# Set 1 of the first mixture as rows by expert, group choice by rank, and a new order of stages

## The chip, the cores and the metric

The kernel runs on one core of a Trainium2 chip. Its time is the device time of one launch in microseconds (us), and the figure compared is the median over several launches. TensorE is called PE here, VectorE DVE, ScalarE ACT, GpSimd POOL, and SyncE SP. SP only issues transfers; ACT and POOL issue some as well.

## The reference

`x` is 32 sequences of 128 positions with 128 features, in f32: 4096 tokens. Six layers are added to it one after the other, each on a layer norm of `x`. The first and the second are an attention and a cross-attention to `ctx`, the fourth and the fifth another attention (with random features) and another cross-attention. The third and the sixth are mixtures of 16 experts:

```python
# third layer: experts of width 64, four groups of four experts
scores = sigmoid(x2d @ router_weight.T)
sc = scores + e_bias
group_scores = sum of the two greatest sc of each group
# only the two best groups count; of them the 4 greatest sc are chosen
tw = 2.5 * scores[chosen] / (sum(scores[chosen]) + 1e-20)
routed = sum over the 4 chosen e of tw_e * (silu(x @ gate_e.T) * (x @ up_e.T)) @ down_e.T
out = routed + shared          # shared: one MLP of width 128 for all tokens

# sixth layer: experts of width 128, the 4 greatest logits, softmax over them, plus a shared MLP
```

## The kernel before

The tokens are eight groups of four sequences (512 tokens). Two groups make a set: set 0 is groups 0 and 1, set 3 is groups 6 and 7. `x` stays on the chip, as [128 positions, 4, 128 features] per group. `fast_decoder` (L960) has four stages: `first_layers` (L1667) with both first attentions of all groups and the experts of group 0 of the first mixture; `mixture_layer` (L2031) with the first mixture of groups 1 to 7; `second_layers` (L2664) with both later attentions; and `last_layer` (L2239) with the second mixture.

**An order written by hand.** `steps` (L1219) takes a list of small pieces of work (a stage, its first step, every how many steps, and how often). Step by step it takes one instruction group from each stage in the order of the list, and between them one from the `between` list. The result is the order of each engine's own queue, and an engine works through it in that order: an instruction that waits holds all behind it on its engine. The order of a list thus decides which queue holds what ahead of what.

**The first mixture, dense.** For each group, `norm`, `scaled` and `turn` make the normalized tokens, once by rows and once turned with the features on partitions (`hx`). `routing` (L1904) computes the router's logits of a set, and `route_groups` (L1797) turns them into weights: sigmoid, the sums of all pairs in each expert group, then `pick` (L1757) for the two best groups and again for the four best experts. `pick` takes the greatest element out k times, six DVE operations each time, breaking ties by a table. The weights go through `send` (L1919) to memory and `fetch` (L1933) brings them back spread over all partitions, four transfers of 512 KB a group. `experts` (L1947) then takes nine chunks per group: eight of two experts (2 x 64 = 128 wide) and the shared MLP. A chunk is three matmuls (`pg`, `pu`, `y`) of 128x512, a Silu on ACT (L1960), and two products on DVE: with `pu` (L1961) and with the spread weights, the share (L1963). The dense chunks compute all 16 experts for all tokens. At most two chunks are in flight, since `pg` and `pu` have four PSUM banks. The sum `y` is copied, turned back (`pyt`) and added to `x`.

**The second mixture.** Its sets 0, 2 and 3 go as rows by expert, through `Tables` (L2089): `route` (L2123) finds the four experts of each token; `placed` (L2160) computes for each token and choice a row in a table in memory, so that the rows of one expert stand together, padded to tiles of 128 rows; `owned` (L2218) finds each tile's expert. `way_out` (L2224) writes the normalized rows to their places: 32 indirect transfers of 128 rows for a set, issued by POOL. Then come 11 quads of four tiles. `rows_of` (L2288) reads a quad's rows and its experts' weights on SP's queue, `rows_turned` (L2304), `rows_up` (L2317) and `rows_down` (L2328) compute them and write the results to a second table. `way_back` (L2337) gathers each token's four results, 32 indirect transfers for a set on POOL, and `added` (L2347) adds them to `x` with their weights on DVE. Set 1 is dense there. Both tables are filled beforehand (`filled`, L2084). At the end `chunk_down` (L2367) computes the last group's shared MLP, adds `x` in the same PSUM sum, copies the 128x512 result (L2378) and sends it out.

**Names in the middle.** While the first mixture ends, pieces of the next attention start: the list `also` (L2031 on). One of them computes on POOL the squares `y2` (L2548), on which the first features of that attention (PE) wait. SP has one queue for all its loads, here: the later weights (L997), `share` (L1943), the weights sent to memory (L1931), and the second mixture's weights (L1026).

Of the kernel before, what the change touches and what calls it, by code (L numbers as in the profile page):

```python
# [9 lines left out]
F32 = mybir.dt.float32  # L10
# [7 lines left out]
GB = 4  # L18
# [57 lines left out]
def _layout(i):  # L76
# [9 lines left out]
    signs, scales = i["L1_attn_sorf_signs"], i["L1_attn_sorf_scales"]  # L86
    pad = lambda a: np.concatenate([a, np.zeros((128 - len(a), a.shape[1]), a.dtype)], 0)
# [68 lines left out]
            "sd": i["L0_ffn_sh_down_w"].T,  # L156
        },
# [802 lines left out]
def fast_decoder(ctx: ExitStack, tc: tile.TileContext, ins, spans, out: bass.AP):  # L960
# [322 lines left out]
    NU = NG * GB  # L1283

# [382 lines left out]
    def first_layers(after):  # L1667
# [15 lines left out]
        rscaled_, rnorm_ = first(rscaled), first(rnorm)  # L1683
        of_four = lambda stage, b, at: (lambda g: stage(g * GB + b), at, 4, NG)
# [3 lines left out]
        def early_keys(s):  # L1688
            for _ in range(early_at[s]):
# [4 lines left out]
        steps(  # L1694
            (lambda k: xvalues(2 * k + 1), 11, 2, NW),
            (weights, 4, 1, NU),
            (lambda k: xvalues(2 * k), (5, 12), 2, EARLY - 1),
            (lambda w: xproject("k", w + EARLY), 8 + 2 * EARLY, 2, NW - EARLY),
# [3 lines left out]
            (lambda g: average(g * GB + GB + 3), 12, 4, NG - 1),  # L1702
            (xweights, (9, 11), 1, NU),
            (finish_, 12, 4, NG - 1),
            of_four(average, 2, 7),
            of_four(average, 0, 5),
            (lambda _: fetch_inside(wk), 41, 1, 1),
            (lambda k: xvalues(2 * (k + EARLY - 1)), 8 + 2 * EARLY, 2, NW - EARLY + 1),
            (first(rturn), 24, 4, NBR // GB),
# [5 lines left out]
            (next_two(rturn), 39, 1, NBR // GB, rscaled_later),  # L1715
            (inside, 42, 1, 2),
            (lambda _: average(3), 7, 1, 1),
            (turn, (3, 7, 11), 4, NG, head_norms),
            (first(send), 39, 1, 1, choose),
            (first(routing), 29, 1, 1),  # L1720
            (finish_first, 7, 1, 1),
            (head_squares, (2, 5, 10), 4, NG, head_means),
            of_four(average, 1, 6),
            (xfinish_b, 13, 2, NW),
            (lambda _: routing(wk, 1), 40, 1, 1),
            (inside, 42, 1, 3),
            (inside, 42, 1, 3),
            (inside, 42, 1, 3),
            (xaverage, (9, 11), 1, NU),
            (xshare, 11, 2, NW),  # L1730
            between=[
                (rnorm_later, 37, 1, NBR // GB),
                (rscaled_later, 38, 1, NBR // GB),
                (xfinish_c, 14, 2, NW),
                (norms, (0, 1, 8, 12), 4, NG),
                (lambda _: choose(1, 12), 41, 1, 3),
                (head_norms, (3, 6, 11), 4, NG),
                (head_means, (2, 5, 10), 4, NG),
                (xnorm, (7, 12), 4, NG, finish_first, finish_),
                (rscaled_, 23, 4, NBR // GB),  # L1740
                (scaled, (1, 2, 9), 4, NG),
                (lambda _: load_w0f(), 21, 1, 1),
                (xscaled, (8, 13), 4, NG),
                (biased, 1, 4, NG),
                (rnorm_, 22, 4, NBR // GB),
                (xnormalize, 12, 2, NW, xweights),
                (lambda k: load_late(LATE[k]), (17, 18), 1, len(LATE)),
                (lambda _: choose(0, 5), 30, 1, 11),
                (filled, 16, 1, NT // 4),
# [6 lines left out]

    def pick(v, n, k, desc):  # L1757

        m = v.shape[1]
        eq = st.tile([128, m, n], F32, name=f"eq{n}", bufs=2)  # L1760
        top = st.tile([128, m], F32, name=f"top{n}", bufs=2)
        for _ in range(k):
            nc.vector.tensor_reduce(top, v, AX.X, ALU.max)
            yield
            nc.vector.tensor_tensor(eq, v, rep(top, n, 2), ALU.is_equal)
            yield
            nc.vector.tensor_tensor(eq, eq, rep(desc, m, 1), ALU.mult)
            yield
            nc.vector.tensor_reduce(top, eq, AX.X, ALU.max)
            yield  # L1770
            nc.vector.tensor_tensor(eq, eq, rep(top, n, 2), ALU.is_equal)
            yield
            nc.vector.scalar_tensor_tensor(v, eq, -BIG, v, ALU.mult, ALU.add)
            yield

    def picked(v):

        nc.vector.tensor_scalar(v, v, -0.1 * BIG, None, ALU.is_lt)
# [18 lines left out]
    def route_groups(lg, wk):  # L1797

        s = wk.tile([128, NBR, E], F32, name="s", bufs=1)
# [14 lines left out]
        yield from pick(gs, 4, 2, K["desc4"])  # L1814
        picked(gs)
# [3 lines left out]
        yield from pick(v, E, 4, K["desc16"])  # L1819
        picked(v)  # L1820
# [10 lines left out]
        comb = wk.tile([128, NBR, E], F32, name="comb", bufs=1)  # L1831
# [19 lines left out]
    def route_softmax(lg, wk):  # L1851

        s = wk.tile([128, NBR, E], F32, name="s", bufs=1)
# [25 lines left out]
        comb = wk.tile([128, NBR, E], F32, name="comb", bufs=1)  # L1879
        nc.vector.tensor_tensor(comb, v, rep(den, E, 2), ALU.mult)  # L1880
        yield
        return comb

    def mixture(tag, W, route, per, last, weights_of, more={}, kept=lambda g: None):
# [14 lines left out]
        def turn(wk, g):  # L1899
            pool, bufs = (edge, 2) if g in groups(0) else (wk, 5)  # L1900
            hs[g] = more[g] if g in more else pool.tile([128, GT], F32, name="hx", bufs=bufs)
            by_feature(xn.pop(g), hs[g])
# [6 lines left out]
        def choose(n, some=-1):  # L1909

            try:
                while some:
                    next(choices[n])
                    some -= 1
            except StopIteration as end:
                if end.value is not None:
                    combs[n] = end.value
# [907 lines left out]
```

## Time and profile before

| what | us |
|---|---|
| median of 11 runs | 1313.91 |
| lowest and highest of them | 1310.22, 1323.21 |
| the profiled execution | 1306.24 |
| its span | 1304.5 |

The stretches of that execution, with the busy time of the engines in each:

| stage | stretch, us | PE | DVE | ACT | POOL | DMA share |
|---|---|---|---|---|---|---|
| first layers | 0 to 597 | 554.7 | 409.6 | 275.5 | 211.8 | 0.24 |
| first mixture, groups 1 to 7 | 597 to 780 | 180.4 | 116.2 | 52.7 | 23.6 | 0.38 |
| second layers | 780 to 1048 | 241.4 | 196.7 | 155.0 | 134.0 | 0.06 |
| second mixture | 1048 to 1304.5 | 229.4 | 132.3 | 106.0 | 165.1 | 0.69 |

Busy time is the time in which an engine executes; a stage lasts as long as its longest chain of waits. The DMA share is the mean busy share of the core's 16 DMA engines. A releaser (`<-`) is the instruction whose end let a waiting one start.

### The profile page before, as it was taken

The numbers are of one execution on the slowest core, as the hardware profiler recorded it, in microseconds if no ns is written. First come the engines' busy times: TensorE is split into PE (matmuls) and PEld (weight loads), VectorE is DVE, ScalarE is ACT, GpSimd is POOL, SyncE is SP. The second block draws the span as 40 slices with busy tenths as digits, with TensorE's granted clock in tenths as the row PEclk, the third lists the DMA queues.
The fourth block names the chain that finished last, engine by engine and source line by source line (L and its number), as shares of the span: only waits on it lengthen the run. The fifth ranks groups of instructions, "written<-read, shape, count | busy, mean of one in ns | idle before, by whom it ended". The sixth has DMA issues, their size and how long they took to land. (4 is left out here: it accounts for less than half of the span.)

```text
span 1304.5 us, 27090 instructions
## 1 busy us (share of the span) xinstructions
PE 1205.8 (92%) x10586; PEld 802.2 (61%) x10586; DVE 854.8 (66%) x2298; ACT 589.2 (45%) x883; POOL 534.5 (41%) x715
## 2 busy tenths in 40 slices
PE   7679999999999999988999998999997788999996
PEld 5357667777777777643443445667665446787753
DVE  5756767686868667576775555688888565524662
ACT  4545454554545443333232224667664433554431
POOL 6244252435352213214000013555543747477774
PEclk9889999999999999999999999999999889999998
DMA  9401221111111112417362301000000157898823
GB/s 327 140 2 34 86 86 34 34 34 34 34 34 34 35 44 57 99 35 163 62 131 57 75 25 80 2 2 2 2 2 8 35 200 263 291 327 282 278 72 94
DMA packets 82751, 118.62 MB, mean 91 GB/s; under 512 B 9016, under 2 KB 57784, under 8 KB 81208
## 3 DMA queue, kind: packets, MB, share of 16 engines
q1 hardware_dynamic: 70280, 92.95, 25.4%
q0 software_dynamic: 6144, 12.60, 3.1%
q10 hardware_dynamic: 6192, 11.26, 2.3%
q8 instruction: 86, 1.41, 0.5%
q14 instruction: 49, 0.40, 0.1%
HBM read 89.71 MB, written 27.07 MB: 90 GB/s over the span
## 5 line engine op out<-in xcount | busy, mean ns | idle before, releaser
L1311 ACT ACTIVATE e<-scores 128x1024 f32<-128x1024 f32 x128 | 124.0, 1021 | 85.4 <-PE scores L981 85.4
L981 PE MATMUL y<-sg,wide 128*128 128x512 f32 x206 | 109.6, 623 | 14.4 <-DVE sg L2365 7.4
L2340 POOL DMA_INDIRECT back<-rows_out,place x96 | 93.4, 973 | 31.1 <-issue 23.5
L1149 POOL TENSOR_SCALAR xn<-x,mv,r 128x128 f32<-128x128 f32 x78 | 69.3, 894 | 84.9 <-PE pxn L1158 79.9
L1565 ACT ACTIVATE e<-xscores 128x1024 f32<-128x1024 f32 x64 | 62.0, 1021 | 65.2 <-PE xscores L981 65.2
L1120 POOL TENSOR_SCALAR r<-mv 128x4 f32<-128x4 f32 x46 | 14.4, 315 | 184.7 <-DVE mv L1139 184.6
L1326 DVE STREAM_TRANSPOSE by_token<-sums 128x512 f32<-128x512 f32 x64 | 45.5, 711 | 66.4 <-PE sums L981 66.1
L1120 POOL TENSOR_SCALAR r2x<-mv 128x2 f32<-128x2 f32 x16 | 3.7, 234 | 203.4 <-DVE mv L1139 203.4
L1960 ACT ACTIVATE sg<-pg 128x512 f32<-128x512 f32 x63 | 37.6, 597 | 107.0 <-PE pg L981 99.1
L981 PE MATMUL scores<-qb,k 32*128 32x512 f32 x512 | 74.7, 654 | 11.2 <-ACT e L1311 7.1
L1961 DVE TENSOR_TENSOR sg<-sg,pu 128x512 f32<-128x512 f32 x63 | 43.2, 686 | 53.3 <-PE pu L981 53.1
L981 PE MATMUL sums<-e,v 128*32 128x128 f32 x2048 | 74.4, 288 | 0.5 <-ACT e L1311 0.5
L981 PEld LDWEIGHTS y<-sg,wide 128*128 128x128 f32 x206 | 34.1, 193 | 63.5 <-DVE sg L1963 29.3
L981 PEld LDWEIGHTS sums<-e,v 128*32 128x32 f32 x2048 | 56.4, 115 | 24.9 <-issue 10.6
L981 PE MATMUL po<-e,v 128*64 128x128 f32 x1024 | 64.9, 277 | 3.8 <-DVE v L1579 3.8
L1613 ACT COPY av<-po 128x512 f32<-128x512 f32 x64 | 37.6, 587 | 64.3 <-PE po L981 63.3
L981 PE MATMUL pqk<-h,wide 128*128 128x256 f32 x256 | 64.5, 397 | 0.7 <-ACT h L1161 0.7
L981 PE MATMUL pval<-wide,ctx 128*128 128x512 f32 x128 | 63.1, 615 | 1.8 <-DVE by_token L1326 1.8
L981 PEld LDWEIGHTS po<-e,v 128*64 128x64 f32 x1024 | 55.1, 137 | 12.3 <-issue 4.2
L1544 DVE COPY qk<-pqk 128x512 f32<-128x512 f32 x54 | 36.8, 685 | 35.6 <-PE pqk L981 35.4
L981 PE MATMUL pu<-hx,wide 128*128 128x512 f32 x116 | 59.3, 593 | 0.0
L981 PE MATMUL pqk<-ctx,wide 128*128 128x256 f32 x256 | 59.3, 384 | 0.0
(355 smaller groups left out, 2955.3 us busy)
## 6 DMA issues: line engine op xcount, KB each, us to landing
row_weights<-in_w1f_dram SPq DMA_DIRECT2D x99, 192.0 KB
factor<-factors SPq DMA_DIRECT2D x64, 256.0 KB
share<-combined SPq DMA_DIRECT2D x28, 512.0 KB
rows_in<-in_few SPq DMA_DIRECT2D x33, 256.0 KB
rows<-rows_in SPq DMA_DIRECT2D x33, 256.0 KB
rows_out<-yrows ACTq DMA_DIRECT2D x33, 256.0 KB
share<-combined SPq DMA_DIRECT2D x8, 1024.0 KB
wide<-in_w1f_dram SPq DMA_DIRECT2D x1, 3272.0 KB
```

What stands on the lines that cost most here:

```text
L981: last[0] = nc.tensor.matmul(*args, **kw)
L1120: nc.gpsimd.tensor_scalar(t, src, add, None, ALU.add)
L1149: eng.tensor_scalar(n[:, b, :], x[g][:, b, :], mv[:, b, 0:1], r[:, b : b + 1], ALU.subtract, ALU.mult)
L1311: nc.scalar.activation(e[-1], ps[:, bass.ts(n, 2)].rearrange("p c i s -> p (c i) s"), AF.Exp, scale=scale)
L1326: nc.vector.transpose(tt.rearrange("p i t r -> p (i t r)"), po.rearrange("p i s -> p (i s)"))
L1544: nc.vector.tensor_copy(t, ps)
L1565: nc.scalar.activation(e[-1], ps[:, n].rearrange("p r c s -> p (r c) s"), AF.Exp, scale=scale)
L1613: nc.scalar.copy(avs[w][n][:, :, bass.ts(b, S)], po)
L1960: nc.scalar.activation(sg, pg, AF.Silu)
L1961: nc.vector.tensor_tensor(sg, sg, pu, ALU.mult)
L2340: nc.gpsimd.indirect_dma_start(out=outs[n, u][:, k], out_offset=None, in_=rows_out[n], in_offset=bass.IndirectOffsetOnAxis(ap=places[n][:, ...
```

## The change

Four things change together.

1. **Set 1 (groups 2 and 3) of the first mixture goes as rows by expert.** `middle_layer` replaces `mixture_layer` and `experts`. It takes 47 dense chunks (five groups of nine, and the shared MLP of groups 2 and 3) and 11 quads. A new array of weights, `w0e`, holds per expert 64 gate columns, 64 up columns and the down matrix twice, one copy in each half of the partitions, 128 KB a tile. Tiles go in pairs: two tiles share a PSUM bank, one in its upper and one in its lower 64 rows, so that one Silu and one product serve both. There are 12 more fills. Group 2's and 3's normalized rows lie in free halves of a weight buffer, which also take the gathered rows later (two rooms).
2. **Groups are chosen by rank** (`pick_groups`): each group's score is compared with all four, ties broken by order, and the count of greater ones must be below 1.5. The four best experts come from `greatest` (eight MAX8 instructions), as in the second mixture. `pick` is gone.
3. **The last group's end**: its shared MLP is added to `x` earlier, and `finish_some` turns, copies and sends `x` of the last group in three parts.
4. **The stages stand in another order** in all four stages, the loads of two small arrays come earlier, and the load of the second mixture's weights waits for the last `added`.

The core of the diff, with the places that the text speaks of:

```diff
+        "w0e": {
+            "gud": np.concatenate(
+                [i["L0_ffn_gate_w"].transpose(2, 0, 1), i["L0_ffn_up_w"].transpose(2, 0, 1), twice], 2
+            ).reshape(128, -1),
+        },
...
-            (next_two(rturn), 39, 1, NBR // GB, rscaled_later),
+            (next_two(rturn), 41, 1, NBR // GB, rscaled_later),
+            (next_four(rturn), 44, 1, NBR // GB, rscaled_last),
-            (first(send), 39, 1, 1, choose),
+            (first(send), 37, 1, 1, choose),
-            (lambda _: routing(wk, 1), 40, 1, 1),
+            (lambda _: routing(wk, 1), 42, 1, 1),
-                (rnorm_later, 37, 1, NBR // GB),
+                (rnorm_later, 39, 1, NBR // GB),
+                (rnorm_last, 42, 1, NBR // GB),
-                (lambda _: choose(1, 12), 41, 1, 3),
+                (lambda _: choose(1, 5), 43, 1, 2),
...
+        g_of, g_by = rep(gs, 4, 3), rep(gs, 4, 2)
+        more_ = pairs[:, :, 0:4].rearrange("p (b q) e -> p b q e", q=4)
+        same = st.tile([128, NBR, E], F32, name=f"eq{E}", bufs=2).rearrange("p b (q e) -> p b q e", e=4)
+        nc.vector.tensor_tensor(more_, g_by, g_of, ALU.is_gt)
+        yield
+        nc.vector.tensor_tensor(same, g_by, g_of, ALU.is_equal)
+        yield
+        nc.vector.tensor_tensor(same, same, rep(before4, NBR, 1), ALU.mult)
+        yield
+        nc.vector.tensor_tensor(more_, more_, same, ALU.add)
+        yield
+        nc.vector.tensor_reduce(gs, more_, AX.X, ALU.add)
+        yield
+        nc.vector.tensor_scalar(gs, gs, 1.5, None, ALU.is_lt)
...
-        yield from pick(v, E, 4, K["desc16"])
+        best = yield from greatest(v)
...
+        def rows_of(n, q):
+            xq = wk.tile([128, 4, D], F32, name="rows", bufs=3)
+            nc.sync.dma_start(out=xq, in_=four_tiles(rows0_in[n], q))
...
+                w = wk.tile([128, 2, S], F32, name="row_weights", bufs=12)
+                src = every[:, bass.ds(e, 1), :].rearrange("p e f -> p (e f)")
+                nc.sync.dma_start(out=w.rearrange("p k f -> p (k f)"), in_=src)
...
+        def rows_up(n, q):
+            h, ws = held[n, q]
+            p = sc([128, 2, 2, S], "pgu")
+            for pair in range(2):
+                for i in range(2):
+                    for r, rows in enumerate(halves):
+                        j = 2 * pair + r
+                        mm(p[rows, i, pair], lhsT=ws[j][:, 0, bass.ts(i, 64)], rhs=h[:, j], start=True, stop=True)
+            sg = wk.tile([128, 2, S], F32, name="sgrows", bufs=2)
+            nc.scalar.activation(sg, p[:, 0], AF.Silu)
+            nc.vector.tensor_tensor(sg, sg, p[:, 1], ALU.mult)
+            held[n, q] = sg, ws
+        def rows_down(n, q):
+            sg, ws = held.pop((n, q))
+            py = [sc([128, 2, D], "pyrows") for _ in halves]
+            for pair in range(2):
+                for r, rows in enumerate(halves):
+                    j = 2 * pair + r
+                    mm(py[r][:, pair], lhsT=sg[rows, pair], rhs=ws[j][rows, 1], start=True, stop=True)
+            y = wk.tile([128, 4, D], F32, name="yrows", bufs=2)
+            for r in range(2):
+                nc.scalar.copy(y[:, r::2], py[r])
+            nc.scalar.dma_start(out=four_tiles(rows0_out[n], q), in_=y)
...
+        def way_back(n, u):
+            outs[n, u] = rooms[u % 2]
+            back_of(tables, rows0_out, n, u, outs[n, u])
+        def added(n, u):
+            add_back(tables, n, u, outs.pop((n, u)))
...
+        dense = [(1, c) for c in range(nch + 1)] + [(2, nch), (3, nch)]
+        dense += [(g, c) for g in range(4, NG) for c in range(nch + 1)]
+        quads = [(n, q) for n in SETS0 for q in range(QUADS)]
+        NQ = len(quads)
+        Q = 11
+        at, todo = {}, list(dense)
+        s = 0
+        while todo:
+            at[s] = [todo.pop(0) for _ in range(min(len(todo), 1 if Q <= s < Q + NQ else 2))]
+            s += 1
+        LAST = max(s + 1, Q + NQ + 1)
...
+        steps(
+            (turn_[3], 5, 1, 1, norm_[3], scaled_[3]),
+            (also[0], 17, 1, 1),
+            (each(rows_turned, quads), Q, 1, NQ),
+            once(fetch, 5, 4),
+            (also[5], 33, 1, 1),
+            (routing_[3], 5, 1, 1),
+            once(tables.owned, n1, 5),
+            once(fetch, 1, 0),
+            (also[4], 27, 1, 1),
+            once(send, 3, 9),
+            once(send, 2, 3),
+            (also[2], 20, 1, 1),
+            (ups, 0, 1, LAST),
+            (downs, 0, 1, LAST),
+            (routing_[2], 0, 1, 1),
+            (ends, 0, 1, LAST + 1),
+            once(fetch, 6, 11),
+            (each(rows_up, quads), Q, 1, NQ),
+            once(fetch, 4, 3),
+            (also[1], 18, 1, 1),
+            (also[3], 22, 1, 1),
+            once(fetch, 7, 17),
+            (each(rows_down, quads), Q + 1, 1, NQ),
+            between=[
+                (scaled_[3], 3, 1, 1),
+                (each(tables.way_out, to_send(n1)), 3, 1, NBR),
+                once(tables.placed, n1, 2),
+                (some_of(3, (10, 10, -1)), 5, 1, 3, routing_[3]),
+                (each(rows_of, quads), Q - 1, 1, NQ),
+                (each(way_back, batches(n1)), Q + QUADS + 1, 1, NBR),
+                (norm_[3], 0, 1, 1),
+                (each(added, batches(n1)), Q + QUADS + 2, 1, NBR),
+                (some_of(n1, (-1,)), 0, 1, 1),
+                (some_of(2, (14, -1)), 0, 1, 2, routing_[2]),
+            ],
+            as_written=0,
+            others=("SP",),
...
+    SETS0 = (1,)
+        for t in (rows0_in if q < QUADS else rows0_out, rows_in if q < QUADS else rows_out):
+            for n in t:
+                nc.sync.dma_start(out=four_tiles(t[n], q), in_=rep(ident, 4, 1))
...
+            if g == NG - 1:
+                nc.vector.tensor_tensor(x[g], x[g], by_token(sgs.pop((g, c)), wd), ALU.add)
+                return
...
+        def finish_some(some):
+            pt = sm([128, len(some), S], "pout")
+            for i, b in enumerate(some):
+                nc.tensor.transpose(pt[:, i], x[NG - 1][:, b, :], ident)
+            t = wk.tile([128, GT], F32, name="y", bufs=2)[:, 0 : len(some) * S]
+            nc.scalar.copy(t, pt.rearrange("p b s -> p (b s)"))
+            nc.scalar.dma_start(out=out[:, bass.ds((NG - 1) * GT + some[0] * S, len(some) * S)], in_=t)
...
             fetch_at(0, 0),
-            (several(each(rows_of, quads), (0, 1)), 0, 1, 1),
+            (each(rows_turned, quads), Q, 1, NQ),
+            (lambda k: finish_some(((0, 1), (2,), (3,))[k]), (53, 54, 56), 1, 3),
+            fetch_at(1, 0),
             fetch_at(4, 3),
-            fetch_at(7, 18),
-            fetch_at(1, 0),
-            (each(rows_turned, quads), Q, 1, NQ),
-            once(tables.owned, n2, 3),
             fetch_at(2, 0),
             fetch_at(5, 9),
             fetch_at(3, 0),
+            once(tables.owned, n2, 3),
             fetch_at(6, 9),
+            (several(each(rows_of, quads), (0, 1)), 0, 1, 1),
             (several(turn, of_set(n3)), 5, 1, 1),
             (ups, 0, 1, LAST),
+            fetch_at(7, 16),
             (each(rows_down, quads), Q + 1, 1, NQ),
             (each(rows_up, quads), Q, 1, NQ),
+            (downs, 0, 1, LAST),
+            (lambda _: not_ok(wk), 29, 1, 1),
             once(tables.owned, n3, 14),
             once(routing, n3, 6),
-            (downs, 0, 1, LAST),
-            (lambda _: not_ok(wk), 29, 1, 1),
             between=[
+                once(tables.placed, n2, 1),
+                (each(way_back, batches(n2)), 29, 1, NBR),
+                once(chosen, n2, 0),
+                once(chosen, n3, 8),
+                (each(added, batches(n3)), 39, 2, NBR),
+                (each(way_back, batches(0)), 18, 1, NBR),
                 once(tables.placed, n3, 9),
-                (each(way_back, batches(n2)), 30, 1, NBR),
-                once(chosen, n3, 8),
-                once(tables.placed, n2, 1),
                 (each(tables.way_out, to_send(n3, 1)), 9, 1, NBR),
-                once(chosen, n2, 0),
-                (each(way_back, batches(n3)), 37, 2, NBR),
+                (each(added, batches(n2)), 30, 1, NBR),
                 once(several(norm, of_set(n3)), None, 3),
-                (each(tables.way_out, to_send(n2, 2)), 1, 1, 4),
-                (each(added, batches(n3)), 39, 2, NBR),
                 (each(rows_of, quads[2:]), Q, 1, NQ - 2),
-                (each(added, batches(n2)), 30, 1, NBR),
+                (each(tables.way_out, to_send(n2, 2)), 2, 1, 4),
                 once(several(scaled, of_set(n3)), None, 4),
-                (each(added, batches(0)), 21, 1, NBR),
-                (each(way_back, batches(0)), 17, 1, NBR),
+                (each(added, batches(0)), 20, 1, NBR),
+                (each(way_back, batches(n3)), 38, 2, NBR),
             ],
             as_written=0,
...
-                (lambda i: tables.way_out(0, to_send[3 * i : 3 * i + 3]), 36, 1, 11),
+                (lambda i: tables.way_out(0, to_send[3 * i : 3 * i + 3]), 38, 1, 11),
-            (lambda _: tables.owned(0), 34, 1, 1),
+            (lambda _: tables.owned(0), 35, 1, 1),
...
+    homes0 = {g: W0X["q"][:, bass.ts(g - 2, GT)].rearrange("p (b f) -> p b f", b=GB) for g in (2, 3)}
+    C = load("last", nc.sync, by_rows)
```

`tables.way_out`, `placed` and `owned` are the ones of before; `tables0.route_groups` is `pick_groups` followed by what `route` does with its choice. `add_back` is the old `added` with other names.

## The prediction

> **What bounds the kernel now.** I read the page first, then the busy time by stretch, then POOL's timeline, then the chain that ended last.
>
> ```profile
> span 1304.5 us, 27090 instructions
> PE 1205.8 (92%) x10586; PEld 802.2 (61%) x10586; DVE 854.8 (66%) x2298; ACT 589.2 (45%) x883; POOL 534.5 (41%) x715
> ```
>
> TensorE is busy for 92% of the span. The share is an average, so the stages decide:
>
> ```profile
> core 0: us, PE busy (x) PEld busy (x) DVE busy (x) ACT busy (x) POOL busy (x), PEclk, DMA share, GB/s
> 597.00:640.00 43.00, 40.77 (x118) 17.72 (x117) 34.61 (x109) 14.78 (x24) 16.35 (x29) 1.00 0.68 144
> 640.00:700.00 60.00, 59.99 (x152) 23.88 (x150) 40.67 (x104) 17.20 (x28) 1.27 (x2) 1.00 0.33 72
> 700.00:740.00 40.00, 40.00 (x101) 16.54 (x101) 19.64 (x31) 10.98 (x19) 1.38 (x2) 1.00 0.51 107
> 1060.00:1110.00 50.00, 45.45 (x217) 28.25 (x216) 30.73 (x96) 18.30 (x34) 29.38 (x31) 0.95 0.78 272
> 1110.00:1170.00 60.00, 57.63 (x401) 47.36 (x401) 26.88 (x70) 32.17 (x57) 35.15 (x36) 1.00 0.93 308
> ```
>
> The first three rows are the first mixture: PE has hardly any idle time there, POOL and the DMA engines have much. The last two are the second mixture, where sets already go as rows by expert: PE idles a little and the DMA engines are nearly full. POOL's timeline of that mixture, with the idle time before each instruction in brackets:
>
> ```profile
> 1126.58 0.96 POOL L2227 DMA_INDIRECT rows_in<-xr,place  x1 [14.48 <-DVE expert_ends L2213]
> 1166.45 1.18 POOL L2227 DMA_INDIRECT rows_in<-xr,place  x1 [0.30 <-issue]
> 1167.94 1.01 POOL L2340 DMA_INDIRECT back<-rows_out,place  x1 [0.30 <-issue]
> 1169.25 0.96 POOL L2340 DMA_INDIRECT back<-rows_out,place  x1 [0.30 <-PE prows L2308]
> ```
>
> A send or a gather takes 0.96 us and 0.30 us of issue: 1.26 us, one after the other. From 1126.6 to the end POOL hardly stops. The chain that ended last shows its end and the tail:
>
> ```profile
> 1289.98 0.94 POOL back L2340
> 1290.93 0.30 issue
> 1291.23 2.49 DMA back<-rows_out,place
> 1293.82 0.36 DVE x L2351
> 1294.51 0.28 DVE sg L2363
> 1294.82 3.79 PE y L981 x10
> 1298.64 0.59 ACT y L2378
> ```
>
> So PE bounds the first mixture, and POOL's indirect transfers the second.
>
> **The change, part by part.**
>
> *PE in the first mixture.* The timeline shows a 128x512 matmul every 0.86 us, so a chunk (pg, pu, y) is 2.58 us. Set 1 loses its 16 expert chunks: 63 become 47, which is -41.3 us. Each of 11 quads adds four transposes (0.43 in this stage), eight matmuls with 64 output rows (0.86 if each takes the 0.107 of a 128x128 one here, half if two run side by side) and four over 64 rows (0.46, or 0.23 by the cross-attention's 32 xscores in 1.86). I take the dearer values, since each pair loads its weights one by one: 1.75 us a quad, 19.3 in all. The places matmuls add 3 us (1056.51 to 1059.4). PE's work falls by about 19 us, and its own end would move from 779.5 to some 769, if the first steps, with two chunks, the norms of group 3 and set 1's tables on VectorE together, cost it 7 to 10 us of waiting (34.6 us of VectorE's work in 43 now, some 12 more then).
>
> [...]
>
> *A new chain for set 1, which ends in POOL.* The stage after the mixture starts when POOL has made the squares y2 (L2548, 782.14 and 783.23, ended 784.27). In the new order of POOL these stand behind all 32 gathers of set 1. So I follow that chain; what else waits behind them on POOL is that pair of squares alone, and PE's features wait for it.
> - First send. In the second mixture the eight MAX8 start at 1042.48 and the first send follows at 1071.48: 29 us. Set 1's MAX8 now fall at the seam of the stages, 597: 626. POOL's last xn before the sends needs a room that a DMA still reads (the combined weights of group 4 and 5), about 3 us by the 2.5 us landing: 629. If the MAX8 come earlier it is 622, if VectorE's crowd of chunks delays them 636.
> - 32 sends at 1.26: 40.3, to 669. Landing 2.5 and the read of the first rows with its issue 3: 675.
> - 11 quads. PE would need 2.58 + 1.75 = 4.33 each, 48 us. The DMA engines carry 11 x (256 KB in, 512 KB of weights, 256 KB out), 11.5 MB, and in the same queue of SP the shares of groups 6 and 7 (two times 2 MB, which stand ahead of the rows of quads 2 and 8): 15.7 MB. At 308 GB/s that is 51 us, at 272 it is 58. I take 53: 728.
> - The last quad lands 3 us later: 731. Then 32 gathers at 1.25, 40 us, and between them what the new order shows: four rotations (0.72), one r and two xn (2.9), four memsets (0.52): 8 us. 779, and y2 twice 1.04: 781.
> That is 3 us before the 784.27 of now. The bounds of the first send and of the transfers make it -17 (622, PE's 48) to +9 (636, 58).
>
> *The clock.* PE would be idle from about 769 until the features start. What such a pause costs is seen at 1053 to 1056 in the trace: PE was busy 1.57 us of 3, and the granted clock was 0.50 from 1058 to 1064 and 0.83 to 1066. That is some 7 us at about half speed, 3.5 us lost at most; little work is there to be slowed, and I take +2 (0 to 3.5). [...]
>
> *Choice by rank.* Per set it takes out 24 operations of 128x128 (0.32 us apart) and 12 of 128x32 (0.22): 10.3 us, and adds the eight MAX8 (0.71) and some eight of 0.3: 3.1. VectorE gains 7 us at each of four sets. It is hidden behind PE in the first mixture, and I cost it at nothing there; without that cover it would be the 7 us, for set 1 counted above in the first send. In the last steps of the first layers (560 to 597) PE was busy 31.6 of 37 us and VectorE 26.4; there norms of groups 4 and 5 come in its place: -1 (-2 to +1). Also there: eight transposes of those groups (0.9 us, in PE's pauses) and the two 32 KB sends of weights a little earlier. Twelve more fills of 256 KB are issued in the first layers behind the old ones, and the next user of the DMA engines comes at 106 us, when the slices show a share of 0 to 0.2: nothing; uncovered, 3.1 MB at 308 GB/s, 10 us. The load of the last weights (3.3 MB, issued at 779.64) now waits for the last added batch; its user is at 1049: nothing.
>
> *The last layer's start.* SP now issues the 1 MB shares ahead of the rows; it did the first at 1048.34 and the other three at 1066.82, with the DMA share at 0.37 between 1048 and 1060. PE starved there behind y and ran at half clock. What counts is when set 3's placing (the 14.48 us wait above) ends. Against it stand the first sends of set 0, moved two steps later: 9 of them, 11 us of POOL that must fit into later steps with POOL two thirds free. I take -1 (-5 to +5).
>
> *The tail.* From the last x (ended 1294.18) to the copy's end (1299.23) were 5.05 us. Now one transpose, a copy of a quarter and the issues: 0.3 + 0.3 + 0.2 = 0.8. -4 (-5 to -3). The share chunk of group 7 goes earlier, into PE's idle time.
>
> *Sum* on the profiled execution (1306.24): -3 + 2 - 1 - 1 - 4 = -7, about 1299. The median of the runs shown lies 7.7 above that execution (1313.91, between 1310.22 and 1323.21), and the prediction is of a median: 1307.
>
> **The rivals.**
> - *PE stays the bound.* The chain above is pessimistic at each joint (sends wait less, transfers overlap); then y2 comes with PE's own end at 769, -15, no pause, and with the other parts -6: 1285, by the median 1293. For it: the DMA share of 0.33 in 640 to 700 leaves room. Against: 32 + 32 transfers on POOL alone are 80 us.
> - *Slower: the rows' chain is late.* Its place is SP's queue: weights of a quad stand behind shares, which wait for rooms that chunks free (SP's longest such wait at L1943 is 9.3 us now), and POOL's gathers wait for the last quad. Price: first send 636 (+7), transfers 58 (+5) and two stalls of 5 (+10): y2 at 803, +19, with the clock 3.5 and the rest -6: +16, by the median 1330. It decides once the chain is 11 us later than I have it, say with quads every 5.4 us (60 instead of 53) and a first send 4 late: that eats the gain and 0.3% more. For it: each link is new and they are in series. Against: the DMA engines of the second mixture hold 308 GB/s with like traffic.
> - *It does not move the time.* The middle comes out even (784) and the last layer's start gives +3, since set 0's later sends hold up its rows: 0 + 2 - 1 + 3 - 4 = 0, 1314. For it: the first quad needs all 32 sends. Against: PE had chunks to fill that time.
>
> **How the numbers follow.** Forecast (middle and seams as summed, 1300 to 1312): 0.45. PE stays the bound: 0.15. Slower: 0.25. No move: 0.15. A measurement of this kernel can tell about 0.3%, 3.9 us, from no change, so faster is below 1310. The forecast puts 0.38 there and 0.07 above; the first rival 0.15; the chain late 0.23 slower and 0.02 same; no move 0.1 same and 0.05 slower. Faster 0.53, same 0.19, slower 0.28. The range takes in the whole first rival and most of the late chain: 1291 to 1326; the forecast's own is 1300 to 1312.
>
> **What would show it.** Right: y2 behind the last gather of set 1, at 775 to 790, with PE idle before it and the clock lowered after; POOL's sends from about 629 without gaps; quads 4.4 to 5.3 us apart; the last copy about 1 us after the last x. Wrong: PE without a pause at 770 (first rival); quads over 5.5 us apart with SP waiting on rooms, or a first send after 636 (the slow one); the last gather of the second mixture not earlier relative to its first send.

## The result, and the profile after

The changed kernel is slower: 1336.36 us median of 12 runs (1328.57 to 1339.43) against 1314.06 for the kernel before (1306.43 to 1323.21). The ratio is 1.0165, with a 95% interval from 1.0147 to 1.0183. Its profiled execution took 1328.2 us, with a span of 1326.4. That is 21.9 above the span of before, about as far apart as the medians, so the two profiles can be compared mark by mark. Both lie some 8 us below their kernel's median; of the changed kernel's 12 runs only two, at 1329 and 1330, are like its profile (granted clock 0.962 and 0.963), and the ten others lie from 1333 up (0.954 to 0.959).

| from | to | before | after | difference |
|---|---|---|---|---|
| start | first chunk of group 1 | 597.2 | 590.6 | -6.6 |
| that | end of the first squares y2 | 187.1 | 212.5 | +25.5 |
| that | first chunk of the last layer | 264.9 | 264.0 | -0.9 |
| that | set 3's first send | 77.4 | 78.2 | +0.7 |
| that | end of the last addition | 167.6 | 173.9 | +6.3 |
| that | end of the span | 10.3 | 7.2 | -3.1 |

The middle lost 25.5 us, the last layer's gathers 6.3, and the rest gained about 10. The page of the changed kernel, its first lines:

```profile
span 1326.4 us, 27889 instructions
PE 1198.4 (90%) x10818; PEld 816.8 (62%) x10818; DVE 840.0 (63%) x2255; ACT 596.3 (45%) x912; POOL 598.3 (45%) x779
```

PE has 7 us less to do by this line, and the span is 22 us longer. The same stretches as before, and two inside them:

```profile
core 0: us, PE busy (x) PEld busy (x) DVE busy (x) ACT busy (x) POOL busy (x), PEclk, DMA share, GB/s
597.00:640.00 43.00, 34.36 (x107) 16.36 (x106) 34.12 (x119) 12.89 (x21) 20.11 (x21) 0.92 0.47 112
640.00:700.00 60.00, 47.97 (x202) 24.31 (x201) 25.16 (x55) 15.50 (x32) 20.32 (x31) 0.91 0.51 145
...
680.00:685.00 5.00, 0.00 (x0) 0.00 (x0) 0.00 (x0) 0.00 (x0) 0.00 (x0) 0.55 1.05 224
685.00:690.00 5.00, 3.00 (x7) 1.92 (x8) 0.00 (x0) 0.73 (x2) 0.00 (x0) 0.50 0.88 303
...
700.00:740.00 40.00, 35.25 (x217) 19.71 (x216) 15.49 (x45) 14.25 (x33) 5.58 (x8) 0.91 0.73 210
```

Where PE had no idle time before, from 640 to 700, it now idles 12 us in 60. From 680 to 685 no engine computes at all, while the DMA engines are full (share 1.05) and move only 224 GB/s. The chain of waits through the middle tells what they moved (start, duration, what), and PE's timeline what PE waited at the first stall:

```profile
673.23 0.64 SPq L1952
673.92 0.60 SPq L1952
674.62 0.57 SPq L1952
675.24 0.61 SPq L1952
675.90 11.05 DMA rows<-rows_in
687.00 1.11 PE prows L2057 x4
...
693.75 0.59 PE prows L2057 x4
698.59 0.59 PE prows L2057 x4
703.42 0.59 PE prows L2057 x4
...
713.43 0.61 SPq L1952
714.09 10.63 DMA rows<-rows_in
724.76 1.00 PE prows L2057 x4
...
687.00 1.11 PE L2057 MATMUL prows<-in_few,rows 128*128 128x128 f32 x4 [9.73 <-DMA rows<-rows_in]
```

L1952 is the fetch of a group's share: four transfers of 512 KB, issued by SP just ahead of the 256 KB of rows of quad 2 (the first is quad 0). The rows land 11.05 us after their issue; quad 8's, behind the next share, after 10.63. PE had other work for a part of that: it waited 9.73 us for quad 2, 2.84 for quad 8 and 1.46 for quad 0. Where no share is in the way, a quad and its chunk take 4.83 us (693.75, 698.59, 703.42).

POOL's timeline, with the first and last transfers of each kind:

```profile
622.96 1.25 POOL L2395 DMA_INDIRECT rows_in<-wide,place  x1 [0.80 <-DVE expert_ends L2381]
663.04 1.06 POOL L2395 DMA_INDIRECT rows_in<-wide,place  x1 [0.30 <-issue]
752.41 1.12 POOL L2007 DMA_INDIRECT wide<-rows_out,place  x1 [22.53 <-DMA rows_out<-yrows]
800.11 0.94 POOL L2007 DMA_INDIRECT wide<-rows_out,place  x1 [0.30 <-issue]
801.08 2.04 POOL L2731 TENSOR_TENSOR y<-y 128x512 f32<-128x512 f32 x2
1145.30 0.96 POOL L2395 DMA_INDIRECT rows_in<-xr,place  x1 [16.00 <-DVE expert_ends L2381]
1247.10 0.94 POOL L2509 DMA_INDIRECT back<-rows_out,place  x1 [5.55 <-DVE x L2520]
1276.21 0.94 POOL L2509 DMA_INDIRECT back<-rows_out,place  x1 [4.25 <-DVE sg L2534]
```

The sends end earlier than forecast and the first gather starts 21 us later; the squares come behind the last gather. In the last layer POOL now stops twice before a gather, 5.55 us for an addition of VectorE that frees a room late, and 4.25 us that the profile puts down to one of VectorE's products (`sg`). And the waits of PE in the middle, by line and releaser (us in total, times, longest):

```profile
PE prows L2057 <- DMA rows<-rows_in: 14.0, 3, 9.7
PE pqphi L988 <- POOL y L2731: 7.0, 1, 7.0
PE y L988 <- DVE sg L2107: 5.8, 2, 5.0
PE qkv L988 <- DVE rot L2717: 3.8, 2, 3.1
```

PE ends the mixture's last chunk at 791, does the first steps of the next attention, and at 795 begins to wait 7.0 us for the squares. The chain that ended last has the new tail:

```profile
1315.86 2.91 DMA back<-rows_out,place
...
1318.86 0.36 DVE x L2520
...
1319.36 0.46 PE pout L2559
...
1319.84 0.27 ACT y L2561
```

### The profile page after: what moved, and what is told of

It reads as the page before. It is cut to its first block, busy times and chain, and to the rows that moved or that the text cites. A ratio compares the mean times of both kernels' runs of the same rounds, so it can differ in the third digit from the quotient of the medians.

```text
span 1326.4 us, 27889 instructions
## 1 busy us (share of the span) xinstructions
PE 1198.4 (90%) x10818; PEld 816.8 (62%) x10818; DVE 840.0 (63%) x2255; ACT 596.3 (45%) x912; POOL 598.3 (45%) x779
## 4 chain that ended last, share of the span: by engine, by line
PE 65%; DVE 10%; POOL 7%; DMA 7%; issue 4%; ACT 4%; SPq 1%; POOLq 0%; ACTq 0%; DVEq 0%
PE pqk L988 8%; PE po L988 7%; PE pu L988 5%; PE pg L988 5%; PE xscores L988 4%; PE scores L988 4%; PE pval L988 4%; PE sums L988 4%; PE y L988 3%; POOL back L2509 3%; PE pyrows L988 2%; PE xsums L988 2%; DMA rows<-rows_in 2%; PE proj L988 2%; PE pS L988 2%
## 5 line engine op out<-in xcount | busy, mean ns | idle before, releaser
L988 PE MATMUL y<-sg,wide 128*128 128x512 f32 x172 | 90.9, 614 | 9.6 <-DVE sg L2107 5.8
L988 PE MATMUL scores<-qb,k 32*128 32x512 f32 x512 | 75.6, 661 | 10.3 <-ACT e L1320 6.0
L2395 POOL DMA_INDIRECT rows_in<-wide,place x64 | 64.0, 1000 | 19.5 <-issue 18.0
L988 PE MATMUL sums<-e,v 128*32 128x128 f32 x2048 | 71.7, 281 | 0.9 <-ACT e L1320 0.9
L2105 DVE TENSOR_TENSOR sg<-sg,pu 128x512 f32<-128x512 f32 x47 | 32.1, 683 | 60.0 <-PE pu L988 57.4
L1156 POOL TENSOR_SCALAR xn<-x,mv,r 128x128 f32<-128x128 f32 x74 | 61.7, 837 | 15.9 <-DMA combined<-xn 15.4
L988 PE MATMUL po<-av,wide 128*128 128x256 f32 x256 | 59.5, 385 | 1.2 <-DVE av L1642 1.2
L1128 POOL TENSOR_TENSOR r<-r,half 128x4 f32<-128x4 f32 x54 | 57.9, 1072 | 4.3
```

The lines of the kernel that those rows point to most:

```text
L988: last[0] = nc.tensor.matmul(*args, **kw)
L1128: nc.gpsimd.tensor_tensor(t, t, halves[exponent].to_broadcast(list(src.shape)), ALU.pow)
L1156: eng.tensor_scalar(n[:, b, :], x[g][:, b, :], mv[:, b, 0:1], r[:, b : b + 1], ALU.subtract, ALU.mult)
L2105: nc.vector.tensor_tensor(sg, sg, pu, ALU.mult)
L2395: sent = nc.gpsimd.indirect_dma_start(out=self.rows[n], out_offset=bass.IndirectOffsetOnAxis(ap=self.places[n][:, k, u : u + 1], axis=0), ...
```

## The experiments

They were run in four batches, each with runs of the kernel before beside it, and each run is compared only with the kernel before, or a control, of its own batch:

| batch | runs | median of the kernel before |
|---|---|---|
| A | shares in parts, last list, rank alone, end alone | 1314.64 |
| B | early squares, all three edits, dense middle (two runs) | 1434.37 |
| C | control, early squares, all three, dense with the old last list | 1313.58 |
| D | dense again, and its three variants | 1436.36 |

In B and D the last layer takes far longer: from set 2's first send to the last addition one and the same kernel took 340 us in B and in D and 227 in C. The expectations call this a slower chip. The record gives B and C the same chip number, so what makes the difference is not shown.

**Shares in parts.** The changed kernel with

```diff
-            once(fetch, 6, 11),
+            (lambda k: made["fetch_part"](wk, 6, k), 12, 1, 4),
-            once(fetch, 7, 17),
+            (lambda k: made["fetch_part"](wk, 7, k), 18, 1, 4),
```

where `fetch_part` issues one of the four 512 KB transfers.

> The changed kernel, with the shares of groups 6 and 7 issued one 512 KB transfer per step among the quads instead of 2 MB at once. Theory: the two waits of about 10.6 us for rows behind the shares make the middle late. Then both waits go, quads come about every 5 us, the squares y2 end near 783 to 788 instead of 803.1, and the median falls from 1336 to 1316 to 1322. Rival: the quads' own traffic of 128 KB weights is what the DMA engines cannot carry; then the parts only spread the same delay, y2 ends at 798 to 803 and the median stays at 1331 to 1336.

Measured: 1320.63 us, 1.0042 of the kernel before [1.0025, 1.0059]. The chain of this run:

```profile
680.11 6.54 DMA rows<-rows_in
...
692.73 6.03 DMA rows<-rows_in
...
722.80 5.49 DMA rows<-rows_in
```

Three loads of rows of about 6 us stand in place of two of 11; the first quad's, with no part ahead of it, took 2.58. PE's wait for rows falls from 14.0 to 6.1 us, and the squares end at 794.4, between the theory's 783 to 788 and the rival's 798 to 803. So the theory is half right: a part still stands ahead of many of the rows. The median fell by 16, as the theory had it, but the profiled span only by 6.9 (1326.4 to 1319.5): this run's profile lies at its median, the changed kernel's 8 us below. Of the 16, the trace accounts for 7 to 9.

**The last layer's list.** The `between` list of `last_layer` as in the kernel before (way_back 17, 30 and 37, added 21, in the old sequence).

> The changed kernel, with the list between the stages of the last layer (gathers, additions, sends, rows) in the order and at the steps of before; its other stages and the last group's new end stay. Theory: the 6.3 us more from set 3's first send to the last addition come from gathers that now wait for rooms behind later additions. Then that stretch falls from 173.9 us to 167 to 169 and the median to 1329 to 1332. Rival: the rows and weights arrive in another order since the shares stand ahead of them; then nothing moves, 1335 to 1338.

Measured: 1331.67, 1.0137 [1.0107, 1.0167], some 4.7 below the changed kernel, though the intervals overlap and the profiled executions are 1.9 apart. The trace is clearer: the stretch fell from 173.9 to 169.3, with 167.6 before, and the wait of the gathers for additions from 6.2 us to 0.6. So the list costs 4.6 of the 6.3 us; the rest stays.

**Choice by rank alone**, in the kernel before: `pick` replaced by the comparison of groups and by `greatest`.

> The kernel before, with the choice by rank alone: groups by comparison, experts by MAX8, everything else and every order as before. Theory: the 6.6 us by which the first layers end earlier in the changed kernel come from VectorE's shorter choice. Then group 1's first chunk starts at 591 to 594 instead of 597.2 and the median is 1307 to 1310. Rival: they come from the new order of the stages; then it starts at 596 to 598 and the median is 1311 to 1315.

Measured: 1312.12, 0.998 [0.9967, 0.9994]; group 1's first chunk at 598.9, later than either had it. The gain is 2.5 us, and the first layers' 6.6 are not from here: the rival holds.

**The new end alone**, in the kernel before: `finish_some`, and group 7's shared part added by token.

> The kernel before, with the last group's new end alone: its shared part is added to x early, and the last quarter is turned, copied and sent by itself. Theory: the time from the last addition to the end of the span falls from 10.3 us to about 7.2, the median by 3, to 1310 to 1312. Rival: the added work ahead (a product by token, one more addition of 128x512 on VectorE) delays the gathers' additions as much; then 1313 to 1315.

Measured: 1309.87, 0.9961 [0.9945, 0.9978], 4.8 us less. From the last addition to the end 6.4 us instead of 10.3.

**Squares early.** The changed kernel with the pieces of the next attention moved up, so that the squares stand ahead of the gathers:

```diff
-            (also[0], 17, 1, 1),
+            (also[0], 12, 1, 1),
...
-            (also[5], 33, 1, 1),
+            (also[5], 20, 1, 1),
```

(the four between them to 13, 14, 16, 18). First in batch B:

> The changed kernel, with the first pieces of the next attention (group 0) five to thirteen steps earlier, so that its squares stand ahead of set 1's 32 gathers in POOL's queue. Theory: PE's own work of the mixture ends at about 792 and then waits some 10 us for the squares behind the gathers; then the features start at 792 to 794, and the median falls by 5 to 10, to 1326 to 1331. Rival: group 1's squares and rotations still stand behind the gathers, and PE waits there instead; then the first features start early but the last layer's first chunk comes no earlier than 1065, and the median stays at 1334 to 1338.

Measured: 1478.23, 1.0325 [1.0271, 1.038]; without the changed kernel beside it, this cannot tell what the edit does. Then with a control, in batch C:

> The changed kernel as it is, beside the next three on one chip: the four runs before it were on a chip whose transfers in the last layer were about a third slower, the kernel before taking 1434 us there. On a chip as the first, 1.015 to 1.018 of the kernel before; on the slower one, 1.03, since the quads' transfers are on its critical path.

> The changed kernel with group 0's squares ahead of set 1's gathers on POOL. Theory: features start up to 10 us earlier and 5 to 10 us of it remain at the end. Rival, which the profile on the slower chip speaks for (first squares at 756.7 there, the next group's only at 837, after the gathers): PE waits for group 1's squares instead and the median is within 3 us of the changed kernel's on the same chip.

Measured: control 1338.65, 1.0212 [1.0176, 1.0248]; with early squares 1327.83, 1.0119 [1.0079, 1.0158]. POOL's timeline of the latter:

```profile
740.68 2.04 POOL L2731 TENSOR_TENSOR y<-y 128x512 f32<-128x512 f32 x2 [17.14 <-ACT y L2729]
759.57 1.12 POOL L2007 DMA_INDIRECT wide<-rows_out,place  x1 [16.85 <-DMA rows_out<-yrows]
```

and PE's waits in the same run:

```profile
PE y L988 <- DVE sg L2107: 12.2, 3, 6.7
PE prows L2057 <- DMA rows<-rows_in: 10.9, 3, 5.4
```

Squares first, gathers after: 10.8 us faster by the medians of four runs each, with intervals that nearly touch, and 3.3 by the profiled executions. PE's wait of 7.0 us for the squares is gone, and PE does not wait for group 1's squares instead, so the rival's place is wrong. But a new wait of 6.7 us stands there, for a product of VectorE. Ahead of such a product VectorE takes a small factor `r`, as the next run shows, and POOL computes that here only from 790.66 to 792.05, behind 24 of its gathers. Against the control's profile the last layer's first chunk comes 6.3 us earlier (1064.7, not 1071.0); the last layer gives a part of that back. PE also waits less for rows (10.9 us, not 16.8), and the moved pieces now stand between the quads. So the edit gains, but what the gathers ahead of the squares cost by themselves is not shown.

**All three edits**, in batch B, then beside the control:

> The three edits together: split shares, squares ahead of the gathers, the list between the last layer's stages as before. If the three costs are separate, the gains add up (16 + 5 to 10 + 5) and the median is 1305 to 1311, below the kernel before. If the gathers are what is left after the shares are split, the early squares only move the wait to group 1, and it is 1314 to 1318, level with the kernel before.

> Split shares, early squares and the last layer's list of before together. Separate costs: 20 to 28 us below the changed kernel on the same chip. If the early squares are worth nothing: about 16 + 5, 19 to 22 below it, and level with the kernel before within 3 us.

Measured: 1471.93, 1.0276 [1.0221, 1.0331] in B; 1311.81, 0.9982 [0.9959, 1.0005] beside the control, 26.8 below it and level with the kernel before. By the medians the single edits gave 16, 10.8 and 4.7, 31.5 in all, so they add up but for 5 us; by the profiled executions 6.9, 3.3 and 1.9, and the three together 15.2. Of what is left, the new wait is seen again on VectorE and PE:

```profile
787.66 0.65 DVE L1156 TENSOR_SCALAR xn<-x,mv,r 128x128 f32<-128x128 f32 x2 [8.43 <-POOL r L1128]
788.24 0.68 DVE L2116 TENSOR_TENSOR sg<-sg,pu 128x512 f32<-128x512 f32 x1
...
789.69 4.15 PE L988 MATMUL y<-sg,wide 128*128 128x512 f32 x4 [7.90 <-DVE sg L2118]
```

VectorE waits 8.43 us for `r`, which POOL computes only between its gathers; behind that wait stand the products of the last dense chunk, and PE waits 7.90 us for those.

**Set 1 dense.** The changed kernel with the dense middle of before, the rest as changed; then also with the old list in the last layer. First in batch B, then beside the control:

> The changed kernel with the first mixture's set 1 dense, in the stages and the order of before (the norms of groups 4 and 5 stay in the first layers, where the change put them); choice by rank, all other orders and the last group's end as changed. Theory: the rows by expert are the whole loss, the other parts are worth 6.6 + 3.1 us less 6.3 in the last layer. Then group 1's first chunk starts at 590 to 593, the squares end 187 us later at 777 to 780, and the median is 1308 to 1312. Rival: the orders of the other stages only pay with the rows; then the middle takes over 190 us and the median is 1314 or more.

> The run before, with the list between the last layer's stages as in the kernel before too. Theory: the stretch from set 3's first send to the last addition falls from 174 to about 169 us and the median is 4 to 5 below the dense run with the changed list, 1303 to 1307, which beats both kernels. Rival: that list costs only where the middle is late; then it is level with the other dense run.

> Set 1 dense in the middle, the last layer's list of before, all else as changed. Theory: the loss is all in the rows by expert and the last layer's list; the first layers' 6.6 and the tail's 3.1 to 3.9 remain as a gain: 8 to 11 us below the kernel before, 1303 to 1306 on a chip as the first. Rival: the first layers' gain is taken back in the middle, 1309 to 1312.

Measured in B: 1430.38, 0.9973 [0.9939, 1.0007], and 1426.92, 0.9958 [0.9929, 0.9987]. The two cannot be told apart there. Beside the control the second took 1295.48, 0.9863 [0.9834, 0.9892]: faster than both kernels, 18 us below the one before and 43 below the changed one, and below the 1303 to 1306 of the theory. Its middle:

```profile
core 0: us, PE busy (x) PEld busy (x) DVE busy (x) ACT busy (x) POOL busy (x), PEclk, DMA share, GB/s
597.00:640.00 43.00, 42.11 (x115) 18.13 (x113) 30.82 (x104) 14.92 (x25) 13.79 (x25) 1.00 0.65 140
640.00:700.00 60.00, 59.79 (x152) 24.26 (x152) 34.00 (x82) 17.41 (x29) 1.27 (x2) 1.00 0.33 71
```

PE is busy throughout, and the middle takes 183.6 us (187.1 before). The size of the gain is less sure than its sign: by the profiled executions it is 8.0 us (3.5 of it in the middle, 3.0 in the second layers, 4.0 at the end; the first layers were no shorter in this one), against the changed kernel 31.7, and the same kernel gained 7 us in batch B.

**Which order has the gain.** Each run takes one order of the dense run back (the whole list of that stage as before; the first also takes back where the middle starts its norms), in batch D. The control is once more the dense kernel with the old last list:

> The dense run with the last layer's list of before once more, beside the three that take one of its orders back on the same chip: 0.984 to 0.989 of the kernel before, 1292 to 1299.

> The dense run with the first layers in the order of before, so that the norms of groups 4 and 5 fall into the middle again (choice by rank stays). Theory: this order is the larger part of what is left beside the new end and the choice by rank. The first chunk of group 1 then starts 4 to 6 us later (597 to 600), the middle takes 187 to 189 us instead of 183.6, and the median rises by 6 to 10, to 1302 to 1306. Rival: it is worth less than 3 us, and the second and last stages have it.

> The dense run with the second layers in the order of before. Theory: the new order there is worth the 3 us by which the profiles differ (261.9 against 264.7 to 264.9 us from the squares to the last layer's first chunk): the median rises by 2 to 4. Rival: it is noise, and nothing moves by more than 1.5.

> The dense run with the last layer's stages in the order of before too (the shares behind the rows again; only the new end stays). Theory: the early shares are worth 0 to 3 us at set 3's first send, as predicted for this step (-1): the median rises by 0 to 3. Rival: the shares ahead of the rows cost time there, and the median falls by 2 or more.

In f1 the old list writes groups 2's and 3's normalized rows where the cross-attention's q weights still lie, so that part of its values differs; the instructions are the same, though the experts that later loads pick need not be. Measured: control 1425.66, 0.9913 [0.9882, 0.9944]; first layers back 1432.24, 0.997 [0.9941, 0.9998]; second layers back 1423.85, 0.9919 [0.9892, 0.9945]; last stages back 1427.28, 0.9923 [0.9895, 0.9951]. By the medians the first layers' order is worth 6.6 us, with intervals that just touch; the other two orders nothing that these runs can tell.

The start of group 1 moved from 592.0 us in the control's profile to 601.8, but that start differs between executions of one kernel. The dense kernel's two other profiles have it at 596.7 (C) and 597.7 (B). The granted clock differs too: in the third of the 40 slices of each page (65 to 97 us in C, 71 to 107 in the others) it was 0.9 or more in the control, 0.8 to 0.9 in B and in f1, and 0.7 to 0.8 in C. So a part of these 9.8 us may be the clock, and the 6.6 rests on the medians.

## Why the prediction was wrong

The forecast was 1307 and faster; the slow rival, at 1330, named the right place. By the prediction's own steps:

- **Eleven quads, 53 us: the step that failed.** Measured 81 us, from the first rows on PE (668.0) to the last quad's results leaving (749.5). The term summed 15.7 MB and divided by 308 GB/s, as if any transfer could run at any time, and put no wait into the quads. SP's transfers were issued in the order of the list, the rows of quads 2 and 8 stood behind 2 MB each and landed 11.05 and 10.63 us after their issue, with the engines full at 224 GB/s and not 308. PE waited 12.6 us for these two. Its queue kept its order too: the dense chunk behind quad 2's rows started only after them (at 687.9), so PE's own end went from the forecast's 769 to 791. The rest of the 28 us, by PE's timeline: some 5 of matmuls at a lower clock (0.50 from 687 to 690, 0.57 from 711 to 713, 0.50 from 725 to 728), some 3.5 of small work between quads, and 7 because the last quad's second products came one step later, behind two dense chunks. Shares in parts gave 8.7 us back at the squares, so the queue is shown for that much; the split of the rest is read from the timeline alone.
- **The 53 itself.** A quad with its chunk took PE 4.83 us without a stall, not 4.33: the side by side pairs take 1.02 and 0.65 us, with 0.59 for the transposes. Eleven of these are 53, so the term agrees with PE's unhindered pace, which is chance: it was made from bytes.
- **The slow rival.** Its two stalls of 5 us are near the 12.6 that PE waited. That its sum for the squares, 803, meets the measured 803.1 is luck: it had the first send at 636, 13 us late, and the quads too short.
- **First send 629:** 622.96. From the MAX8 (601.37) it took 21.6 us, not the 29 of the second mixture, so the row was too dear. **32 sends, 40.3:** 40.1 to the last one's start. So the rows reached PE at 668, not 675, which hid 7 us of the quads' loss.
- **Gathers and what lies between them, 48, and the squares, 2:** 50.7, from 752.41 to 803.12. That they stand ahead of the squares was read rightly: PE waited 7.0 us there. The sum for the squares was 781, measured 803.1: the 22 us are the quads' 28 less the early start.
- **The first steps' 7 to 10 us of PE waiting:** 8.6 idle in 597 to 640. Right.
- **The clock, +2:** the price of one pause was about right, the number of pauses was not. At the first stall the clock fell to 0.55 (680 to 685) and 0.50 (685 to 690), and PE's first pair of matmuls afterwards took 1.71 us, where the same pair takes 0.86; it was back to full within 4 us of PE's restart (0.61 from 690 to 691, then 1.00), with 1.9 us lost, where the term had 2 and 3.5 at most. The clock was low also after the wait of 2.84 us (0.50 from 725 to 728). The term had one such pause; the trace has six places with a clock of 0.50 to 0.57 (PE restarts or slows at 611, 687, 711, 725, 776 and 802), and the matmuls there took some 13 us longer than their like, by an estimate from the same trace. How much of it lay on the critical path is not shown.
- **First layers, -1:** -6.6 in the profile. The choice by rank alone is worth 2.5 us by the medians; the order, with the norms of groups 4 and 5 moved into PE's pauses, 6.6 (f1), with intervals that just touch. Its mechanism was named, its size too small.
- **The last layer's start, -1:** +0.7; taking it back changed nothing measurable. The term was right to be small. What it did not cost is the gathers' order in the same list, +6.3, of which the old list gives 4.6 back in the trace. The prediction treated the steps of way_back and added as no change at all.
- **The tail, -4:** -3.1 in the profile, -3.9 in the end alone, whose median fell by 4.8. Right.

So the change holds two things of opposite sign. The rows by expert cost some 38 us by the medians (43 less the last list's 5) and some 30 by the profiled executions (31.7 less 1.9). The rest with the old list gains 18 in batch C, and 7 and 11 in B and D. That PE has less to do was read rightly (19 us by the sum; 7 by the page, where a matmul at a lower clock counts with all of its time, as the pair of 1.71 us instead of 0.86 does); it was worth nothing while PE stood behind rows.

What stays open: after the three edits the rows still cost 16 us against the dense middle (1311.81 and 1295.48, both in batch C). By the profile the wait for `r` behind the gathers is 8 of them; no run took it away, so that is argued and not shown. Two edits that follow from the lines above were not run either: the rows issued ahead of the shares, and more rooms for rows.

## What to carry to other kernels

Do not price transfers by their sum over a bandwidth when one in-order queue issues them: price the small load that is needed next, behind the largest one put ahead of it (here 256 KB of rows landed after 11.05 us behind 2 MB, and, in the run with shares in parts, after 2.58 with none ahead), and ask how many buffers it can be ahead. Work taken off the bounding engine can be lost again to what stands in that engine's queue in its place: here PE had some 19 us less to do by the sum, and waited 9.73 us for the rows of quad 2 with a dense chunk next in its queue. And when a change has several parts, run them apart before judging it: here the parts around the main one were worth 0.4 to 1.4 per cent, and with the main one they were lost. Before you trust a gain of a few microseconds, look at how far two profiles of one and the same kernel lie apart.

## What was not expected

The DMA engines were full at 224 GB/s while they spread the shares over the partitions, and reached 303 (after, 685 to 690) and 308 (before, 1110 to 1170) in stretches with a lower share, 0.88 and 0.93: a full share of the engines is no bandwidth. Batches differ by 9% on the same kernel (1314 and 1434 us), most of it in the last layer, with its indirect transfers and loads by expert. In the slower batch the version with more of such transfers did worse: the three edits together were at 0.998 of the kernel before in batch C and at 1.028 in batch B. So a version is best compared with one run beside it; why the batches differ stays open.
